# Last stage of a gated two-layer kernel: the choice of experts on 32 partitions, spread through DRAM, in place of TensorE transposes and pair products

## The chip, the cores and the metric

The kernel runs on one core of a Trainium2 chip. A core has five engines with their own instruction streams: TensorE (PE; its weight loads are shown apart as PEld), VectorE (DVE), ScalarE (ACT), GpSimd (POOL) and SyncE (SP), which here does nothing but issue DMA transfers, in order. Tensors lie in SBUF (128 partitions) or, for the results of TensorE, in PSUM banks. The metric is the device time of one execution in microseconds; lower is better.

## The reference, cut to what matters

All of it is float32, for 16 sequences ("batches") of 256 tokens with 256 channels. Two layers follow one another, each with a cross attention and a feed-forward part, each part added to `x` with a gate. The change concerns only the last part, a gated linear attention with a dense and a sparse half:

```python
e = jax.nn.softmax(x @ We, axis=-1)                   # 4 experts per token
_, idx = lax.top_k(e, 1)
mask = jax.nn.one_hot(idx, N_EXP, dtype=x.dtype).sum(-2)
rw = e * mask
fac = jnp.swapaxes(rw, 1, 2)[:, :, :, None, None]
mfac = jnp.swapaxes(mask, 1, 2)[:, :, :, None, None]
q_e = q2[:, None] * fac
k_e = k2[:, None] * fac
gk_e = gk2[:, None] * mfac
o_dense = gla_b(q1, k1, v, gk1)                       # chunked, causal
o_sparse = gla_be(q_e, k_e, v, gk_e).sum(axis=1)      # one attention per expert
o = o_dense + o_sparse
```

A pair of tokens (s, t) contributes to the sparse half only where both chose the same expert, and then with the product of the two tokens' probabilities; the decay (`gk_e`) between them sums only over tokens of that expert.

## The kernel before, in words

The kernel works through four stages, one per part, each with a loop over the 16 batches. The last one, `stage3_fast`, is a generator. Its first steps (for batch 0) are run between the steps of the stage before; then it runs a loop over p = 0 to 63, four quarters (m = 0 to 3) for each of 16 batches. Each quarter makes the keys, queries, decays and products of two heads of the dense and two of the sparse half. The instructions of this stage stay in the order in which the Python code issues them, on each engine; tables (`start`, `middle`, `rest`, `late`, `behind_mask`, `by_rows`, `logs`) name by quarter which preparatory step for the next batch is issued at which place of the quarter.

For the choice of experts of batch b + 1, made during batch b, these are:

- quarter 0: `lows` multiplies the normed tokens (`xnT`) with all low-rank weights and the four expert columns, so that PSUM holds the logits as rows 81 to 84, tokens along the free axis, and VectorE copies it to `low`. `route_rows` turns these rows with two TensorE transposes into a spare corner of the bank `sc`, so that tokens lie on partitions: 128 partitions, 2 token halves, 4 experts. `route_logits` subtracts the largest and takes the exponential, `route_sums` the reciprocal sum.
- quarter 1: `route` multiplies by it and finds the first largest of the 4 (ties are broken by `prio`, which falls from 4 to 1 along the experts), and writes `hots`: the probability at the chosen expert, 0 elsewhere.
- quarter 2: `turn_hot` turns `hots` with two TensorE transposes into 4 rows (`hT`), `turned_hot` copies them to SBUF.
- start of quarter 3: `pairs` multiplies `hT` with itself on TensorE (`both`, 256 + 128 columns). An entry is the product of two tokens' probabilities if they chose the same expert, else 0. VectorE makes two masks of it: `em` (is it above 0, times the decay mask `dmask`) and `am` (times the causal mask `amask`).

`em` is the moving operand of the `gz` products (`decays`), first needed for p + 1 in quarter 3. `am` is multiplied into the sparse products (`masked`, n = 1) from the next batch on.

Other work that these steps stand next to: `turn_ahead` (quarter 2) turns the normed tokens of batch b + 2 in 32x32 squares on VectorE into the tile `turned`, and SyncE puts the squares in place with 16 transfers into `xnT`, which `lows` reads in quarter 0 of the next batch. `norms` (quarter 1) sends the 8 rows of normalizing factors through DRAM (`rms`) and back, repeated over partitions (`r`, two transfers). `outgates` leaves copies in the tile tag `zs`. `steepest` reduces the logarithms of the gates (`gates`) in quarter 3, `project` multiplies with the output weights there (`proj`), and VectorE adds the result to `x`. There is one bank `sc` for the products: TensorE may write the next ones when VectorE's `at` has read the last.

In the profile all operations of VectorE, ScalarE and GpSimd in this stage carry line 50 (a helper), and TensorE's lines 1637 (matmul) and 1640 (transpose), so they are told apart by the names of their tiles.

Of the kernel before, what the change touches and what calls it, by code (L numbers as in the profile page):

```python
# [73 lines left out]
def layers(ctx: ExitStack, tc: tile.TileContext, t, out, check):  # L74
# [1544 lines left out]
    def stage3_fast(early_bank):  # L1619

        with ExitStack() as sx:
# [29 lines left out]
            hots = [w1.tile([P, 2, 4], F32, tag=f"hot{n}", name=f"hot{n}") for n in range(2)]  # L1651
# [43 lines left out]
            def lows(b):  # L1695

                low[b] = of(b).tile([P, 2, S], F32, tag="low", name="low")
                ps = bank("low")
                for c in range(2):
                    for k in range(2):  # L1700
                        matmul(ps[:, c * S:(c + 1) * S], la[:, k, c * P:(c + 1) * P], xnT[b][:, k, :],
                                         start=k == 0, stop=k == 1)
                dve3.tensor_copy(low[b][:, 0, :], ps[:, :S])
                dve3.tensor_scalar(low[b][:, 1, :], ps[:, S:], vec[:, V_ONE:V_ONE + 1], None, ALU.add)
                lowd[b] = of(b).tile([P, S], F32, tag="lowd", name="lowd")
                nc.sync.dma_start(out=lowd[b][64:], in_=low[b][:64, 1, :])
                if b > 0:
                    nc.sync.dma_start(out=low2, in_=low[b][64:, 1, P:])

            e_, den_, z_ = {}, {}, {}  # L1710

            def route_rows(b, ps):

                for i in range(2):
                    transpose(ps[:, 64 * i:64 * i + 64], low[b][64:P, 1, tokens(i)], ident[64:P, 64:P])
                z_["rt"] = ps

            def route_logits(b):

                ps = z_.pop("rt")  # L1720
                src = ps.rearrange("p (i e) -> p i e", i=2)[:, :, 17:21]
                mx = st.tile([P, 2], F32, tag="emx", name="emx")
                dve.tensor_reduce(mx, src, AX.X, ALU.max)
                e = e_[b] = st.tile([P, 2, 4], F32, tag="e", name="e")
                dve.tensor_tensor(e, src, bc(mx, [P, 2, 4], 2), ALU.subtract)
                act.activation(e, e, AF.Exp)

            def route_first(b):
                route_rows(b, bank("rt")[:, :P])
                route_logits(b)  # L1730

            def route_sums(b):
                den = den_[b] = st.tile([P, 2], F32, tag="eden", name="eden")
# [3 lines left out]
            def route(b):  # L1737
                e, shape = e_.pop(b), [P, 2, 4]
                dve.tensor_tensor(e, e, bc(den_.pop(b), shape, 2), ALU.mult)
                m, q, c = (st.tile(x, F32, tag=n, name=n) for n, x in (("em", [P, 2]), ("eq", shape), ("ec", [P, 2])))  # L1740
                dve.tensor_reduce(m, e, AX.X, ALU.max)
                first = bc(prio[:, 4:], shape, 1)
                dve.tensor_tensor(q, e, bc(m, shape, 2), ALU.is_equal)
                dve.tensor_tensor(q, q, first, ALU.mult)
                dve.tensor_reduce(c, q, AX.X, ALU.max)
                dve.tensor_tensor(q, q, bc(c, shape, 2), ALU.is_equal)
                dve.tensor_tensor(hots[b % 2], q, e, ALU.mult)
# [34 lines left out]
            def turn_hot(b):  # L1782
                ps = bank("hT")
                for i in range(2):
                    transpose(ps[:4, tokens(i)], hots[b % 2][:, i, :], ident)
                z_[b, "hot"] = ps

            def turned_hot(b):
                hT[b] = of(b).tile([4, S], F32, tag="hT", name="hT")
                dve3.tensor_copy(hT[b], z_.pop((b, "hot"))[:4, :S])  # L1790

            def pairs(b):

                x, both = hT.pop(b), bank("both")
                matmul(both[:, 0:S], x[:, :P], x, start=True, stop=True)
                matmul(both[:, S:3 * P], x[:, P:], x[:, P:], start=True, stop=True)
                em[b] = of(b).tile([P, 2, P], F32, tag="em", name="em")
                dve3.scalar_tensor_tensor(em[b], both.rearrange("p (i s) -> p i s", i=2)[:, :, :P], 0.0, dmask,
                                          ALU.is_gt, ALU.mult)
                am[b] = of(b).tile([P, 384], F32, tag="am", name="am")  # L1800
                dve3.tensor_tensor(am[b], both[:, :384], amask, ALU.mult)
# [104 lines left out]
            def products(p, n):  # L1906
# [4 lines left out]
                if n == 0 and m == 0 and b + 1 < B:  # L1911
                    route_rows(b + 1, ps[:, 1, 384:])
# [121 lines left out]


            start = {3: [(pairs, 1)]}
            middle = {0: [(lows, 1)], 1: [(all_gates, 1)], 2: [(turn_hot, 1)], 3: [(scaled_first, 0)]}

            rest = {0: [(bias, 2)], 2: [(turned_hot, 1), (norm_ahead, 2)], 3: [(steepest, 1, 0), (steepest, 1, 1)]}
# [15 lines left out]
            for group in (((bias, 0), (stats, 0)), ((norm, 0),), ((turn, 0),), ((lows, 0),), ((gates, 0, 0),),  # L2055
                          ((gate_logs, 0, 0), (route_first, 0)), ((route_sums, 0), (gates, 0, 1)),
# [6 lines left out]
            for f, *a in ((turn_hot, 0), (turned_hot, 0), (stats, 1), (pairs, 0), (norm, 1), (steepest, 0, 0),  # L2063
                          (steepest, 0, 1)):
                f(*a)
# [185 lines left out]
```

## Time and profile before

| | us |
|---|---|
| time, median of 3 runs | 1832.49 (1831.44 to 1832.76) |
| the profiled execution's own time | 1833.27 |
| its span, first to last instruction | 1831.5 |
| TensorE busy | 1793.7 |
| GpSimd busy | 1015.0 |
| VectorE busy | 1137.3 |
| ScalarE busy | 832.2 |

The granted TensorE clock was 0.997 of full speed. The last stage begins at about 1222 us of the span and takes about a third of it, 36.75 us for a batch. How to read the lines: in a view in order of time, the first number is the start from the beginning of the span, the second the time taken, then the engine, the line, the operation, output and inputs by tile name, their shapes (partitions x elements) and the number of instructions merged; in brackets the idle time of that engine before it and the instruction that ended it. In the chain that ended last, each piece is what the next one waited for, followed back from the last instruction of the kernel. TensorE's instructions run pipelined, and their ends are modelled, so they overlap in these lists.

### The profile page before, as it was taken

What the parts mean: (1) busy time and instruction counts of PE and PEld (TensorE: products, weight loads), DVE (VectorE), ACT (ScalarE), POOL (GpSimd) and SP (SyncE); (2) the same over time, 40 slices, a digit from 0 to 9 for tenths busy, and PEclk for the clock granted to TensorE, in tenths of its full rate; (3) what the DMA queues carried; (4) which work ended last, traced back from release to release, by engine and by line L of the source; (5) the groups of instructions that cost most, each with busy time, mean ns of one, the idle gap of its engine ahead of it and who ended that gap; (6) DMA issues with size and microseconds to landing.
All of it is one profiled execution on the core that took longest, in us unless ns stands there. A gap on an engine that the chain in (4) does not pass through costs nothing.

```text
span 1831.5 us, 35425 instructions
## 1 busy us (share of the span) xinstructions
PE 1793.7 (98%) x13930; PEld 1242.3 (68%) x13930; DVE 1137.3 (62%) x2695; ACT 832.2 (45%) x1727; POOL 1015.0 (55%) x1001
## 2 busy tenths in 40 slices
PE   8999999999999999999999999998999999999997
PEld 5666666666666666666777866656777777777775
DVE  3345656666656666666475388866666666666664
ACT  4433335343443334534343388754544454445432
POOL 3654766567666677656643866313454445444533
PEclk9999999999999999999999999999999999999999
DMA  9800010000010100000067933100111111111110
GB/s 303 231 1 22 16 35 13 28 17 16 31 35 10 30 20 10 28 24 17 13 207 244 256 64 50 24 3 11 35 30 36 29 31 34 34 31 27 38 31 26
DMA packets 110361, 98.05 MB, mean 54 GB/s; under 512 B 43835, under 2 KB 97763, under 8 KB 109673
## 3 DMA queue, kind: packets, MB, share of 16 engines
q1 hardware_dynamic: 97897, 78.91, 14.5%
q0 software_dynamic: 12288, 16.79, 4.5%
q8 instruction: 112, 1.84, 0.4%
q14 instruction: 64, 0.52, 0.1%
HBM read 52.03 MB, written 38.41 MB: 49 GB/s over the span
## 4 chain that ended last, share of the span: by engine, by line
PE 81%; DVE 7%; POOL 7%; ACT 2%; issue 2%; DMA 1%; SPq 0%; POOLq 0%; DVEq 0%; ACTq 0%
PE o L50 12%; PE qk L50 11%; PE v L50 9%; PE sc L50 8%; PE proj L50 7%; PE sc L1637 5%; PE kq L1637 5%; POOL es L50 4%; PE gq L1637 3%; PE v L1637 3%; PE proj L1637 3%; PE ex L50 3%; DVE at L50 2%; PE o L1637 2%; POOL rs L50 2%
## 5 line engine op out<-in xcount | busy, mean ns | idle before, releaser
L50 POOL TENSOR_SCALAR rs<-mv 128x2 f32<-128x2 f32 (+2 forms) x85 | 16.3, 191 | 398.3 <-DVE mv L50 396.5
L50 DVE RECIPROCAL rd<-o 128x256 f32<-128x256 f32 x64 | 112.3, 1755 | 155.9 <-PE o L50 155.9
L50 ACT ACTIVATE e<-sc 128x1024 f32<-128x1024 f32 (+1 forms) x192 | 181.6, 1016 | 18.4 <-PE sc L50 18.4
L50 POOL TENSOR_TENSOR at<-at,at 128x768 f32<-128x768 f32 x63 | 114.2, 1812 | 133.5 <-DVE at L50 133.5
L50 PE MATMUL sc<-qk 64*128 64x256 f32 (+1 forms) x1536 | 183.1, 384 | 0.5 <-DVE qk L50 0.5
L50 PE MATMUL o<-e,v 128*32 128x256 f32 (+1 forms) x3072 | 177.9, 379 | 0.0
L50 PEld LDWEIGHTS sc<-qk 64*128 64x128 f32 (+1 forms) x1536 | 132.0, 172 | 55.1 <-issue 26.8
L50 POOL TENSOR_TENSOR esum<-esum,es 128x512 f32<-128x512 f32 x128 | 163.4, 1277 | 10.0
L50 PE MATMUL qk<-kvT,wkv 128*128 128x333 f32 x512 | 164.3, 443 | 0.0
L50 POOL TENSOR_TENSOR es<-e 128x1024 f32<-128x1024 f32 x64 | 151.3, 2364 | 12.0 <-ACT e L50 9.0
L50 ACT ACTIVATE qk<-qk 128x256 f32<-128x256 f32 x128 | 48.8, 382 | 231.7 <-PE qk L50 231.7
L50 POOL TENSOR_TENSOR es<-es,e 77x1024 f32<-77x1024 f32 x64 | 150.3, 2349 | 5.0
L50 DVE TENSOR_TENSOR at<-sc,amask 128x768 f32<-128x768 f32 x64 | 61.3, 958 | 135.1 <-PE sc L1637 79.6
L50 PEld LDWEIGHTS o<-e,v 128*32 128x32 f32 (+1 forms) x3072 | 99.9, 110 | 66.2
L50 PE MATMUL qk<-kvT,wq 128*128 128x256 f32 x512 | 134.6, 385 | 0.0
L50 DVE COPY qk<-qk 128x333 f32<-128x333 f32 x128 | 64.6, 505 | 94.8 <-ACT qk L50 93.3
L50 POOL DMA_INDIRECT x<-rows_out,pos x64 | 100.9, 1577 | 35.8 <-issue 18.7
L50 PEld LDWEIGHTS qk<-kvT,wq 128*128 128x128 f32 x512 | 94.3, 189 | 35.1 <-issue 9.6
L50 PEld LDWEIGHTS qk<-kvT,wkv 128*128 128x128 f32 x512 | 97.2, 190 | 30.0
L50 PE MATMUL proj<-wo0h,oT 128*128 128x256 f32 x512 | 113.7, 380 | 0.3 <-DVE oT L50 0.3
L50 PE MATMUL v<-wkv,kvT 128*128 128x512 f32 x256 | 113.1, 595 | 0.0
L50 PEld LDWEIGHTS proj<-wo0h,oT 128*128 128x128 f32 x512 | 95.9, 190 | 13.9 <-issue 0.8
(267 smaller groups left out, 3919.5 us busy)
## 6 DMA issues: line engine op xcount, KB each, us to landing
rows<-zero SPq DMA_DIRECT2D x16, 640.0 KB
xin<-rows SPq DMA_DIRECT2D x16, 640.0 KB
r<-rms SPq DMA_DIRECT2D x30, 256.0 KB
rows_out<-y SPq DMA_DIRECT2D x16, 384.0 KB
v<-vctx SPq DMA_DIRECT2D x15, 308.0 KB
x<-in_x_dram SPq DMA_DIRECT2D x16, 256.0 KB
rows_out<-y SPq DMA_DIRECT2D x16, 256.0 KB
out_dram<-x SPq DMA_DIRECT2D x15, 256.0 KB
```

Of the source, the lines that this page charges most:

```text
L50: x = getattr(self.engine, name)(*a, **k)
L1637: tc.keep_in_program_order(nc.tensor.matmul(*a, **k))
```

## The change

The logits stay on 32 partitions. After `lows`, VectorE turns the 32 rows that hold the logits in 32x32 squares (`rl`, in a tile of the tag `turned`), so that a lane holds 8 tokens with 4 experts each. The choice is made there, on 32 lanes with 32 elements, and gives two numbers for each token: its largest probability (`w`) and the code of the expert that has it (`c`, from `prio`). One more VectorE transpose of a 32x32 square lays them out as rows, and a transfer writes them to DRAM (`picks`, 2 x 256 numbers). From there two transfers read them back: `rows`, both rows repeated on all 128 partitions (256 KB), and `cols`, where each partition gets the four numbers of its own two tokens.

The masks are then made on VectorE alone. `same` compares `c` along the free axis with `c` of the partition's own token and multiplies with `dmask`: two instructions of 128 elements. `weights` makes `am` as (same choice) times w, then times the own w and `amask`: four instructions, two of 256 and two of 128 elements. `pairs`, `turn_hot`, `turned_hot`, `route_rows` and the `hots` tiles are gone, with their TensorE and VectorE instructions. `same` stands where `pairs` stood, at the start of quarter 3, and `weights` after the two `steepest` reductions of quarter 3. For batch 0, at the start of the stage, `steepest` comes before `same` and `weights`, and the norm of batch 1 after them.

```diff
-            hots = [w1.tile([P, 2, 4], F32, tag=f"hot{n}", name=f"hot{n}") for n in range(2)]
+            choice, chosen = (w1.tile([P, 32], F32, tag=n, name=n) for n in ("choice", "chosen"))
+            nc.gpsimd.memset(choice, 0.0)
...
                 dve3.tensor_scalar(low[b][:, 1, :], ps[:, S:], vec[:, V_ONE:V_ONE + 1], None, ALU.add)
+                rl[b] = w1.tile([P, 4, P], F32, tag="turned", name="rl")[:, :2, :].rearrange("p x d -> p (x d)")
+                dve3.transpose(rl[b][64:96, :], ps[64:96, S:])
...
-            def route_rows(b, ps):
-
-                for i in range(2):
-                    transpose(ps[:, 64 * i:64 * i + 64], low[b][64:P, 1, tokens(i)], ident[64:P, 64:P])
-                z_["rt"] = ps
+            picks = [tc.dram_tile([2, S], F32, name=f"picks{b}") for b in range(B)]
+            few, own_rows = [32, 8, 4], slice(64, 96)
...
             def route(b):
...
-                dve.tensor_tensor(q, q, bc(c, shape, 2), ALU.is_equal)
-                dve.tensor_tensor(hots[b % 2], q, e, ALU.mult)
+                dve.transpose(chosen[own_rows], choice[own_rows])
+                nc.sync.dma_start(out=picks[b].rearrange("n (k a) -> (n k) a", a=32), in_=chosen[64:80])
+                x = w2.tile([P, 512], F32, tag="zs", name="rows") if b else w0.tile([P, 2, D], F32, tag="xn", name="rows")
+                rows[b] = x.rearrange("p (n s) -> p n s", n=2) if b else x
+                nc.sync.dma_start(out=rows[b], in_=bc(picks[b], [P, 2, S], 0))
+                cols_[b] = w1.tile([P, 2, 2], F32, tag="cols", name="cols")
+                nc.sync.dma_start(out=cols_[b], in_=picks[b].rearrange("n (i p) -> p n i", p=P))
...
-            def turn_hot(b):
-                ps = bank("hT")
+            def same(b):
+
+                em[b] = of(b).tile([P, 2, P], F32, tag="em", name="em")
                 for i in range(2):
-                    transpose(ps[:4, tokens(i)], hots[b % 2][:, i, :], ident)
-                z_[b, "hot"] = ps
-
-            def turned_hot(b):
-                hT[b] = of(b).tile([4, S], F32, tag="hT", name="hT")
-                dve3.tensor_copy(hT[b], z_.pop((b, "hot"))[:4, :S])
-
-            def pairs(b):
-
-                x, both = hT.pop(b), bank("both")
-                matmul(both[:, 0:S], x[:, :P], x, start=True, stop=True)
-                matmul(both[:, S:3 * P], x[:, P:], x[:, P:], start=True, stop=True)
-                em[b] = of(b).tile([P, 2, P], F32, tag="em", name="em")
-                dve3.scalar_tensor_tensor(em[b], both.rearrange("p (i s) -> p i s", i=2)[:, :, :P], 0.0, dmask,
-                                          ALU.is_gt, ALU.mult)
-                am[b] = of(b).tile([P, 384], F32, tag="am", name="am")
-                dve3.tensor_tensor(am[b], both[:, :384], amask, ALU.mult)
+                    dve3.scalar_tensor_tensor(em[b][:, i, :], rows[b][:, 1, tokens(i)], cols_[b][:, 1, i:i + 1],
+                                               dmask[:, i, :], ALU.is_equal, ALU.mult)
+
+            def weights(b):
+
+                w, c = (rows[b][:, n, :] for n in range(2))
+                x = am[b] = of(b).tile([P, 384], F32, tag="am", name="am")
+                for i, (lo, hi) in enumerate(((0, S), (S, 3 * P))):
+                    dve3.scalar_tensor_tensor(x[:, lo:hi], c[:, i * P:], cols_[b][:, 1, i:i + 1], w[:, i * P:],
+                                               ALU.is_equal, ALU.mult)
+                    dve3.scalar_tensor_tensor(x[:, lo:hi], x[:, lo:hi], cols_[b][:, 0, i:i + 1], amask[:, lo:hi],
+                                               ALU.mult, ALU.mult)
...
-                if n == 0 and m == 0 and b + 1 < B:
-                    route_rows(b + 1, ps[:, 1, 384:])
...
-            start = {3: [(pairs, 1)]}
-            middle = {0: [(lows, 1)], 1: [(all_gates, 1)], 2: [(turn_hot, 1)], 3: [(scaled_first, 0)]}
-
-            rest = {0: [(bias, 2)], 2: [(turned_hot, 1), (norm_ahead, 2)], 3: [(steepest, 1, 0), (steepest, 1, 1)]}
+            start = {3: [(same, 1)]}
+            middle = {0: [(lows, 1)], 1: [(all_gates, 1)], 3: [(scaled_first, 0)]}
+
+            rest = {0: [(bias, 2)], 2: [(norm_ahead, 2)], 3: [(steepest, 1, 0), (steepest, 1, 1), (weights, 1)]}
...
-            for f, *a in ((turn_hot, 0), (turned_hot, 0), (stats, 1), (pairs, 0), (norm, 1), (steepest, 0, 0),
-                          (steepest, 0, 1)):
+            for f, *a in ((stats, 1), (steepest, 0, 0), (steepest, 0, 1), (same, 0), (weights, 0), (norm, 1)):
```

More of the change, by code (lines that the diff above doesn't have):

```diff
@@ L1708, in lows, with small @@
                     nc.sync.dma_start(out=low2, in_=low[b][64:, 1, P:])
-            e_, den_, z_ = {}, {}, {}
-            def route_rows(b, ps):
-                for i in range(2):
-                    transpose(ps[:, 64 * i:64 * i + 64], low[b][64:P, 1, tokens(i)], ident[64:P, 64:P])
-                z_["rt"] = ps
+            e_, den_, z_, rl, rows, cols_ = {}, {}, {}, {}, {}, {}
+            picks = [tc.dram_tile([2, S], F32, name=f"picks{b}") for b in range(B)]
+            few, own_rows = [32, 8, 4], slice(64, 96)
+            def small(name, shape):
+                return w1.tile([P] + shape[1:], F32, tag=name, name=name)[own_rows]
             def route_logits(b):
-                ps = z_.pop("rt")
-                src = ps.rearrange("p (i e) -> p i e", i=2)[:, :, 17:21]
-                mx = st.tile([P, 2], F32, tag="emx", name="emx")
+                src = rl.pop(b)[own_rows].rearrange("p (k c) -> p k c", c=32)[:, :, 17:21]
+                mx = small("emx", few[:2])
                 dve.tensor_reduce(mx, src, AX.X, ALU.max)
-                e = e_[b] = st.tile([P, 2, 4], F32, tag="e", name="e")
-                dve.tensor_tensor(e, src, bc(mx, [P, 2, 4], 2), ALU.subtract)
+                e = e_[b] = small("e", few)
+                dve.tensor_tensor(e, src, bc(mx, few, 2), ALU.subtract)
                 act.activation(e, e, AF.Exp)
-            def route_first(b):
-                route_rows(b, bank("rt")[:, :P])
-                route_logits(b)
             def route_sums(b):
-                den = den_[b] = st.tile([P, 2], F32, tag="eden", name="eden")
+                den = den_[b] = small("eden", few[:2])
                 dve.tensor_reduce(den, e_[b], AX.X, ALU.add)
@@ L1737, in route @@
             def route(b):
[L1738 to L1744, printed above, removed]
-                dve.tensor_reduce(c, q, AX.X, ALU.max)
-                dve.tensor_tensor(q, q, bc(c, shape, 2), ALU.is_equal)
-                dve.tensor_tensor(hots[b % 2], q, e, ALU.mult)
+                e, q = e_.pop(b), small("eq", few)
+                w, c = choice[own_rows, :8], choice[own_rows, 8:16]
+                dve.tensor_tensor(e, e, bc(den_.pop(b), few, 2), ALU.mult)
+                dve.tensor_reduce(w, e, AX.X, ALU.max)
+                dve.tensor_tensor(q, e, bc(w, few, 2), ALU.is_equal)
+                dve.tensor_tensor(q, q, bc(prio[own_rows, 4:], few, 1), ALU.mult)
+                dve.tensor_reduce(c, q, AX.X, ALU.max)
+                dve.transpose(chosen[own_rows], choice[own_rows])
[5 more added lines that the diff above has]
+                nc.sync.dma_start(out=cols_[b], in_=picks[b].rearrange("n (i p) -> p n i", p=P))
             def gates(b, i):
@@ L2055, in stage3_fast @@
             for group in (((bias, 0), (stats, 0)), ((norm, 0),), ((turn, 0),), ((lows, 0),), ((gates, 0, 0),),
-                          ((gate_logs, 0, 0), (route_first, 0)), ((route_sums, 0), (gates, 0, 1)),
+                          ((gate_logs, 0, 0), (route_logits, 0)), ((route_sums, 0), (gates, 0, 1)),
                           ((route, 0), (vals, 0), (gate_logs, 0, 1), (bias, 1))):
```

## The prediction

> **What bounds the kernel now.** I read the page's busy times, the chain that ended last over one batch of the last stage, then VectorE, SyncE and TensorE in order of time over that batch.
>
> ```profile
> PE 1793.7 (98%) x13930; PEld 1242.3 (68%) x13930; DVE 1137.3 (62%) x2695; ACT 832.2 (45%) x1727; POOL 1015.0 (55%) x1001
> ```
>
> TensorE is busy 98% of the span: work taken from it is worth its time, unless something else was nearly as late. The chain over 1487 to 1525 (start us, us, what):
>
> ```profile
> 1495.54 0.27 PE sc L1640
> ...
> 1496.69 0.96 DVE at L50
> 1497.65 0.08 DVE emx L50
> ...
> 1497.95 0.21 ACT e L50
> ...
> 1498.68 1.29 DVE zs L50 x2
> ...
> 1500.57 1.30 DVE at L50 x4
> ...
> 1501.91 0.70 PE sc L1637 x2
> ...
> 1509.62 0.22 PE hT L1640 x2
> ...
> 1517.11 0.84 PE both L1637 x4
> ```
>
> A batch takes 36.75 us (`low` starts at 1492.74 and 1529.50). The three routing pieces of TensorE (turned logits 0.27, `hT` 0.22, `both` 0.84) all lie on the chain. In quarter 0 the chain leaves TensorE for VectorE, through the routing operations `emx`, `e` and `eden`, and comes back at 1501.91. VectorE in quarter 3 (idle time before, and its releaser, in brackets):
>
> ```profile
> 1517.22 0.41 DVE L50 TENSOR_TENSOR q<-gq,ee 128x256 f32<-128x256 f32 x1
> 1517.99 0.42 DVE L50 SCALAR_TENSOR_TENSOR em<-both,dmask 128x256 f32<-128x256 f32 x1 [0.37 <-PE both L1637]
> 1518.34 0.55 DVE L50 TENSOR_TENSOR am<-both,amask 128x384 f32<-128x384 f32 x1
> 1518.80 1.38 DVE L50 SCALAR_TENSOR_TENSOR at<-sc,kden,am 128x256 f32<-128x256 f32 x4
> 1520.10 0.68 DVE L50 TENSOR_TENSOR u<-o,gw 128x512 f32<-128x512 f32 x1
> 1520.70 2.33 DVE L50 TENSOR_REDUCE gates<-lg 128x1 f32<-128x1024 f32 x2
> 1524.27 0.75 DVE L50 SCALAR_TENSOR_TENSOR x<-proj,gate,x 128x512 f32<-128x512 f32 x1 [1.24 <-PE proj L1637]
> ```
>
> It has 1.24 us of air before `x<-proj`. SyncE, and the TensorE instruction its sixteen `xnT` transfers are for:
>
> ```profile
> 1508.42 1.32 SPq L1998 DMA_DIRECT2D r<-rms  x2
> ...
> 1516.79 10.33 SPq L1693 DMA_DIRECT2D xnT<-turned  x16
> ```
> ```profile
> 1272.12 1.97 PE L1637 MATMUL low<-xnT,la 128*128 128x256 f32 x8 [1.68 <-DMA xnT<-turned]
> ...
> 1529.50 1.89 PE L1637 MATMUL low<-xnT,la 128*128 128x256 f32 x8
> ```
>
> The last issue ends at 1527.12, `low` starts 2.38 us later. Where `low` did wait, it started 1.37 to 1.54 us after the last issue (1270.58 to 1272.12, 1748.92 to 1750.29): I take 1.4, so the usual slack is about 0.98 us. This second path, from VectorE's `turned` over SyncE to the next `low`, decides how much of the gain can be kept.
>
> **The change part by part.** The sum is made against the profiled execution's 1833.27 us (span 1831.5), 0.78 above the median of 1832.49.
>
> *Quarter 0 (15 batches).* The turned logits leave TensorE: -0.27. VectorE's new 32x256 transpose sits between the `low` copies (end 1495.48) and `at`; priced by `dens` (128x256, 0.44) it ends at 1495.9, before `at` can start at 1496.42: hidden, with its cover 0.5 us. If it weren't, `at` would be late one for one. The small operations now have 32 elements a lane in place of 8. From 128 to 256 elements `at` goes from 342 to 472 ns, about 1 ns an element, so 24 elements cost 25 ns each for `emx`, `e`, `eden`; the exponential 20 (128x8 is 208); the reciprocal goes from 166 ns (2 elements) to 244 (16), 5.6 ns an element, so 34 for 6 more. They follow one another on the chain: +0.13. Net -0.14, ends -0.27 (nothing added) and 0 (twice as much added). 15 x 0.14 = 2.1.
>
> *Quarter 1.* `route` loses two operations of 0.19 and gains 25 ns on five and a 32x32 transpose (128x64 takes 0.239): the same end within 0.1 us. GpSimd waits for the `mv` behind it, but its `at` sum ends 0.6 us before TensorE's `o` at 1515.03: nothing. SyncE gets three issues: `picks` waits for `chosen`, `rows` for the landing of `picks`, `cols` follows. Queued behind them are only the sixteen `xnT` issues at 1516.8, and SyncE is free from 1509.74.
>
> *Quarter 2.* `hT` leaves TensorE: 15 x 0.22 = 3.3. TensorE runs without a pause from there to `sc`, and the 0.40 VectorE copy lay in idle time.
>
> *When do rows and cols land?* `rms` (8 KB to DRAM) took 1.74 us from issue to release. `picks` is issued at 1509.74 behind the two `r` transfers, whose data flows until 1512.4, so it lands at about 1512.9. `rows` (256 KB) then starts moving about 1.4 us after its issue (as `r` did) and takes half of what the two `r` took, 1.2: until 1515.5. `cols` is 512 pieces of 4 bytes, 32 on each of the 16 DMA engines. No row has 4-byte pieces. Lower end: the first load, `vec`, has pieces of 72 bytes, 143 packets in 9.5% of 16 engines over 1 us, 10.6 ns each: 0.35 us. Upper end: `r` with 1 KB pieces, 512 packets in 2.6 us at 0.69 of 16 engines, 56 ns: 1.8 us. With 0.45 us to release, `cols` is there between 1516.3 and 1517.8. I take the lower end, `vec` being the nearest in size. VectorE reaches `same` at 1517.41 (its `q`, 0.22 earlier).
>
> [...]
>
> *Quarter 3, TensorE.* `both` goes: -0.84. *VectorE* loses `em` and `am` (0.97 together and 0.37 of waiting). New: operations with a lane scalar cost 0.342 (128 elements) and 0.472 (256); independent ones start 0.09 before the last ends, dependent ones 0.03 after. `same`: 2 x 0.25 = 0.50. `weights`: 0.50 + 0.38 + 0.37 + 0.25 = 1.5. From 1517.41: GpSimd's `u` product still runs until 1517.57, and I let `same` wait for it, because both its operands lie in SBUF: earlier, `rq<-re,prio` of one form ran from 160 to 2189 ns, one of them (888.60, 1.07 us) ending with GpSimd's pair of sums (887.03, 2.62 us). Then 1517.57 + 0.50 + `at` 1.30 + `u` 0.60 + `gates` 2.33 + 1.5 = 1523.8. `x<-proj` could start at 1523.19, so it is 0.6 late; `at` ends at 1525.44, just when TensorE wants its `sc` bank (1525.44). So VectorE's air is used up, and nothing is lost yet; any further lateness of `same` is paid one for one.
>
> [...]
>
> *Quarter 3, what is late next.* `turned` comes before `both`, so its landing doesn't move, while `low` would come 0.84 earlier. Slack per batch (end of the last issue to `low`, less 1.4): seven batches 0.91 to 0.99, six with longer issuing (10.65 to 11.35 us) 0.51, 0.66, 0.41, 0.27, 0.03 and 0; the first has none (it waits 1.68 already). The last batch has no `low`. Kept: 7 x 0.84 + 1.9 + 0 + 0.84 = 8.6 of 12.6. Ends: 12.6 if SyncE is never late, 4 if its 3 more issues a batch lengthen the seven too.
>
> *Start of the stage.* Route ends at 1220.2 now and `em` at 1226.34. Then: 0.26 earlier without the turned logits, picks 1.74, rows 0.65 + 1.4 + 1.2, cols 0.35 + 0.45, landing near 1225.8, while `gates`, now ahead, ends near 1226.2. `em` ends at 1226.7, +0.3 with ends -0.3 and +1.0 (`cols` at 56 ns). `weights` and `xn` behind it (2.2 us) end before TensorE's `tr` at 1231.
>
> Sum: 2.1 + 3.3 + 8.6 - 0.3 = 13.7. 1833.27 - 13.7 = 1819.6, on the median's scale 1818.8.
>
> **The rivals.**
> - *All of it.* The transfers of `xnT` keep up: 15 x (0.14 + 0.22 + 0.84) - 0.3 = 17.7, giving 1814.8 (1812.8 with nothing added to the small operations). For it: seven batches still have 0.14 us over. Against it: six have less than 0.84.
> - *VectorE is the bound in quarter 3.* `weights` blocked by GpSimd or dearer, or `cols` at its upper end (1517.8, 0.2 late): 0.2 to 0.8 us a batch. The first 0.14 hides under the `xnT` slack; 1820 to 1829.
> - *Slower: the 4-byte pieces are dear.* `same` waits for `cols`, VectorE stands, and `gz` and the `sc` bank are late. A batch gains 0.36 before it and 0.84 in it, so it decides from 1.2 us of lateness: landing 1518.8, (1518.8 - 0.45 - 1515.5) / 32 = 89 ns a piece. At 100 ns the landing is 1519.15, 1.6 late, 0.4 lost a batch: 1832.5 + 6 + 0.3 = 1839. For it: no row shows such a piece. Against it: both priced rows lie below.
> - *The pieces leave TensorE and nothing shortens*: excluded, since they lie on the chain without a pause.
>
> **How the numbers follow.** Forecast 0.50 (1815.5 to 1821); all of it 0.12 (1812 to 1815.5); VectorE the bound 0.19 (1821 to 1829); slower or near no change 0.19 (0.03 of it within 0.2%, which is 3.7 us and about what a measurement can tell). The range 1812.5 to 1829 leaves out the last case. Faster 0.78, same 0.04, slower 0.18.
>
> **What would show it.** Right: no `both`, `hT` or turned logits; batches of about 35.7 to 36.0 us; `low` waiting for `xnT` in some; `same` starting within 0.2 us of `q`'s end; `x<-proj` with no idle time before it. Wrong: VectorE's `em` waiting for `cols` by a microsecond or more; `cols`' issue on SyncE well above 0.7 us; TensorE idle at the second `sc` of quarter 3; `xnT` issues starting later than 0.1 us after `turned`.

## The result: 0.23% slower

| | before | after |
|---|---|---|
| time, median of 8 runs each, one chip (us) | 1832.11 (1828.88 to 1834.36) | 1836.56 (1834.65 to 1838.77) |
| ratio to before, 95% interval | | 1.0023 [1.0013, 1.0033] |
| the profiled execution's own time | 1833.27 | 1837.53 |
| its span | 1831.5 | 1835.7 |
| granted TensorE clock | 0.997 | 0.995 |

The forecast was 1818.8 us, with a range of 1812.5 to 1829: too low by 17.8 us, with the sign wrong. TensorE did lose the work: between the second batch's `low` and the last one it was busy 504.09 us before and 492.21 after, but that stretch took 514.41 us before and 519.12 after. So its idle time there grew from 10.3 to 26.9 us. The busy times on the page of the kernel after:

```profile
PE 1778.2 (97%) x13802; PEld 1226.5 (67%) x13802; DVE 1165.8 (64%) x2743; ACT 834.1 (45%) x1727; POOL 1014.6 (55%) x1002
```

Four marks on TensorE divide a batch: the first `low`, the first of the gate products (`sc<-lbg`, whose bank VectorE's `at` has to free), the first `v`, the first `proj`, and the next `low`. Summed over the 13 batches that have all five, in us:

| kernel | low to gate products | to v | to proj | to next low | sum |
|---|---|---|---|---|---|
| before | 119.46 | 112.63 | 130.44 | 115.64 | 478.17 |
| after | 125.21 | 109.74 | 124.51 | 122.62 | 482.08 |
| difference | +5.75 | -2.89 | -5.93 | +6.98 | +3.91 |

With the batch before these (36.24 to 37.04, +0.80) and what follows the last `low` (81.2 to 80.7, -0.5), that is the 4.2 us between the spans. Two stretches gain, two lose more. The clock does not explain it: the granted clock is 1.00 over these 13 batches in both executions. In the batch before them it is 0.50 for 3.41 us after the change (1268.93 to 1272.34), and from `den` to `low` takes 4.0 us there instead of 2.4; before, `low` waited 1.68 us for `xnT` in that batch, so the two nearly cancel.

Of the 3.91 us, 3.0 fall in two neighbouring batches of after (37.74 and 38.79 us in place of 36.76), which the last section looks at: in each, a packet of 16 KB of the queue `q8 instruction` moved (for 1.28 and 1.43 us) while a transfer was on its way. In the other eleven, gains and losses nearly cancel: 0.9 us in all.

**The first stretch.** The chain that ended last, kernel after, at the same place as the lines of before (start us, us, what):

```profile
1494.59 1.97 PE low L1637 x8
...
1498.41 0.97 DVE at L50
...
1504.25 0.70 PE sc L1637 x2
```

The turned logits, `hT` and `both` are gone; the path over VectorE, through `emx`, `e` and `eden`, is still there, and longer. From `low` to `at` it is 3.82 us (3.95 before, 1492.74 to 1496.69), but from `at` to the gate products 5.84 (5.22 before, 1496.69 to 1501.91). VectorE itself in order of time, kernel before and kernel after:

```profile
1496.69 0.96 DVE L50 TENSOR_TENSOR at<-sc,amask 128x768 f32<-128x768 f32 x1 [1.21 <-PE sc L1637]
1497.56 0.15 DVE L50 TENSOR_REDUCE emx<-sc 128x2 f32<-128x8 f32 x1
1497.75 0.17 DVE L50 TENSOR_TENSOR e<-sc,emx 128x8 f32<-128x8 f32 x1
1497.84 0.68 DVE L50 TENSOR_TENSOR f<-kq,ee 128x512 f32<-128x512 f32 x1
```
```profile
1498.41 0.96 DVE L50 TENSOR_TENSOR at<-sc,amask 128x768 f32<-128x768 f32 x1 [0.53 <-PE sc L1637]
1499.40 0.18 DVE L50 TENSOR_REDUCE emx<-rl 32x8 f32<-32x32 f32 x1
1499.62 0.18 DVE L50 TENSOR_TENSOR e<-rl,emx 32x32 f32<-32x32 f32 x1
1499.83 0.69 DVE L50 TENSOR_TENSOR f<-kq,ee 128x512 f32<-128x512 f32 x1
...
1501.92 0.41 DVE L50 TENSOR_TENSOR q<-gq,ee 128x256 f32<-128x256 f32 x1
1502.36 0.18 DVE L50 TENSOR_REDUCE eden<-e 32x8 f32<-32x32 f32 x1
1502.57 0.19 DVE L50 RECIPROCAL eden<-eden 32x8 f32<-32x8 f32 x1
1502.80 1.39 DVE L50 SCALAR_TENSOR_TENSOR at<-sc,kden,am 128x256 f32<-128x256 f32 x4
```

The small operations themselves cost next to nothing more (0.18 and 0.19 in place of 0.15 to 0.17). What is new is at the seams: `emx` starts 0.03 us after `at` ends, `f` 0.03 after `e`, `eden` 0.03 after `q`, `at` 0.04 after the reciprocal. None of these pairs depends on one another, and in the kernel before they overlapped by 0.08 to 0.09 (`at` 1496.69 + 0.96 = 1497.65, `emx` at 1497.56; `e` 1497.75 + 0.17 = 1497.92, `f` at 1497.84). At just these four places the operations change between tiles that begin at partition 64 and tiles that begin at partition 0.

**The end of a batch.** SyncE in order of time, kernel after, one batch (its `low` began at 1420.47):

```profile
1436.62 1.33 SPq L1994 DMA_DIRECT2D r<-rms  x2
1438.04 0.55 SPq L1744 DMA_DIRECT2D picks<-chosen  x1
1442.11 0.35 SPq L1747 DMA_DIRECT2D rows<-picks  x1
1442.51 0.43 SPq L1749 DMA_DIRECT2D cols<-picks  x1
1444.78 11.27 SPq L1694 DMA_DIRECT2D xnT<-turned  x16
```

TensorE and VectorE in the quarter 3 that follows:

```profile
1444.29 0.82 PE L1637 MATMUL sc<-q,k 64*128 64x256 f32 x8
1445.35 1.13 PE L1637 MATMUL kq<-xnT,wk 128*128 128x256 f32 x4 [0.24 <-DVE f L50]
1448.07 3.62 PE L1637 MATMUL proj<-wo,u 128*128 128x256 f32 x16
...
1457.64 1.97 PE L1637 MATMUL low<-xnT,la 128*128 128x256 f32 x8 [0.38 <-DMA xnT<-turned]
```
```profile
1444.02 0.70 DVE L50 STREAM_TRANSPOSE turned<-xn 128x512 f32<-128x512 f32 x1
1444.64 0.65 DVE L50 TENSOR_TENSOR f<-kq,ee 128x512 f32<-128x512 f32 x1
1445.22 0.41 DVE L50 TENSOR_TENSOR q<-gq,ee 128x256 f32<-128x256 f32 x1
1445.93 0.61 DVE L50 SCALAR_TENSOR_TENSOR em<-rows,cols,dmask 128x128 f32<-128x128 f32 x2 [0.30 <-DMA cols<-picks]
...
1452.18 0.75 DVE L50 SCALAR_TENSOR_TENSOR x<-proj,gate,x 128x512 f32<-128x512 f32 x1
1452.84 0.95 DVE L50 TENSOR_TENSOR at<-sc,amask 128x768 f32<-128x768 f32 x1
```

Three things are late here. `kq` waits for `f`, which has to free the only `kq` bank and stands behind `turned`; while `both` stood in front of `kq`, it gave `f` that time. `em` waits for `cols`. And `low` waits for the transfers of `xnT`: from `turned` to `low` it takes 13.62 us here (1444.02 to 1457.64) and 13.48 in the kernel before (1479.26 to 1492.74). With 23.28 us from `low` to `turned` before (1455.98 to 1479.26) the path adds up to the period of 36.76, as it must; what counts is the slack in it. Before, the sixteen issues took 10.34 us and ended 2.38 us ahead of `low`, of which about 1.4 is needed (so much where `low` did wait). After, the path is 23.55 (1420.47 to 1444.02) + 13.62 = 37.17: the issues take 11.27 us and end 1.59 us ahead of `low` (1456.05 to 1457.64), so no slack is left. Whatever TensorE gained behind `turned` cannot shorten that.

### The profile page after: what moved, and what is told of

Its sections match the earlier page's. It is cut to its first block, busy times and chain, and to the rows that moved or that the text cites. A ratio compares the mean times of both kernels' runs of the same rounds, so it can differ in the third digit from the quotient of the medians.

```text
span 1835.7 us, 35258 instructions
## 1 busy us (share of the span) xinstructions
PE 1778.2 (97%) x13802; PEld 1226.5 (67%) x13802; DVE 1165.8 (64%) x2743; ACT 834.1 (45%) x1727; POOL 1014.6 (55%) x1002
## 4 chain that ended last, share of the span: by engine, by line
PE 73%; DVE 10%; POOL 7%; DMA 2%; ACT 2%; issue 2%; SPq 2%; DVEq 0%; POOLq 0%; ACTq 0%
PE o L50 11%; PE qk L50 11%; PE v L50 9%; PE sc L50 8%; PE proj L50 7%; PE sc L1637 5%; PE kq L1637 4%; POOL es L50 4%; DVE at L50 3%; PE ex L50 3%; PE v L1637 2%; PE gq L1637 2%; PE proj L1637 2%; PE low L1637 2%; POOL rs L50 2%
```

## The experiments

The theory at this point: (1) the change of partitions costs VectorE's overlap, 0.6 us a batch on the way to the gate products; (2) the transfers of `xnT` eat what is gained behind `turned`; (3) if they are made faster, VectorE's `f` and its lateness in quarter 3 come next. Rivals: the small operations are dear for their shape; the wait for `cols` is the cause; the two DRAM steps slow everything that SyncE issues. All runs below have the kernel before timed beside them on the same chip (medians 1830.92 to 1832.35 us); the groups ran on four chips, so runs of different groups are best compared by their ratios or by the sums over the 13 batches.

### Choice on partitions 0 to 31

```diff
-                dve3.transpose(rl[b][64:96, :], ps[64:96, S:])
+                dve3.transpose(rl[b][0:32, :], ps[64:96, S:])
...
-            few, own_rows = [32, 8, 4], slice(64, 96)
+            few, own_rows = [32, 8, 4], slice(0, 32)
...
-                nc.sync.dma_start(out=picks[b].rearrange("n (k a) -> (n k) a", a=32), in_=chosen[64:80])
+                nc.sync.dma_start(out=picks[b].rearrange("n (k a) -> (n k) a", a=32), in_=chosen[0:16])
```

> The changed kernel, with the choice on partitions 0 to 31 in place of 64 to 95 (the transpose of the logits writes there). Theory 1: quarter 0 got slower (from `low` to the gate products 9.66 us in place of 9.17) because VectorE stops overlapping two operations whenever the first partition changes between 0 and 64, which it does four times on that path at 0.11 to 0.12 us. Then this stretch falls to about 9.2 us, the `f` after `e` starts before `e` has ended again, and the time falls by 15 x 0.46 = 6.9 us, to about 1829.7. Rival: the small operations cost that much because of their 32 elements a lane or because both operands lie in SBUF; then the stretch stays at 9.6 and the time at 1836.5.

Measured: 1826.15 us, ratio 0.9970 [0.9958, 0.9981]: faster than before. From `low` to the gate products: 117.66 us in the 13 batches (9.05 each), in place of 125.21. The stretch gains 0.58 us a batch where 0.46 had been expected. The time is 3.5 us below the expected 1829.7; this explains 1.8 of it, and the rest is not explained. VectorE in order of time in this run:

```profile
1313.26 0.96 DVE L50 TENSOR_TENSOR at<-sc,amask 128x768 f32<-128x768 f32 x1 [0.53 <-PE sc L1637]
1314.13 0.16 DVE L50 TENSOR_REDUCE emx<-rl 32x8 f32<-32x32 f32 x1
1314.33 0.18 DVE L50 TENSOR_TENSOR e<-rl,emx 32x32 f32<-32x32 f32 x1
1314.44 0.67 DVE L50 TENSOR_TENSOR f<-kq,ee 128x512 f32<-128x512 f32 x1
...
1316.49 0.41 DVE L50 TENSOR_TENSOR q<-gq,ee 128x256 f32<-128x256 f32 x1
1316.82 0.16 DVE L50 TENSOR_REDUCE eden<-e 32x8 f32<-32x32 f32 x1
1317.02 0.19 DVE L50 RECIPROCAL eden<-eden 32x8 f32<-32x8 f32 x1
1317.14 1.33 DVE L50 SCALAR_TENSOR_TENSOR at<-sc,kden,am 128x256 f32<-128x256 f32 x4
```

The same instructions with the same shapes, and the four seams overlap again by 0.07 to 0.09 us: `at` to the next `at` takes 3.88 us in place of 4.39. The four seams alone are 0.13 + 0.31 = 0.44 of that 0.51. Shape was not the cause, the start partition was: with the change between 64 and 0 the four pairs stood 0.03 to 0.04 us apart, without it they overlap. No run tried the choice on other partitions.

### Four of the sixteen transfers of xnT issued by ScalarE

```diff
-                for q in range(0, P, 32):
+                for q in range(0, 96, 32):
...
+            def turn_rest(b):
+                to, y = z_.pop((b, "turned"))
+                for r in range(0, P, 32):
+                    tc.keep_in_program_order(nc.scalar.dma_start(out=to[r:r + 32, :, 96:], in_=y[96:, :, r:r + 32]))
...
-                    2: [(gate_logs, 1, 1), (normed_out, -1, 0), (normed_out, -1, 1)]}
+                    2: [(gate_logs, 1, 1), (turn_rest, 2), (normed_out, -1, 0), (normed_out, -1, 1)]}
```

Three kernels carry this edit: after with it, after with it and partitions 0 to 31, and before with it.

> The changed kernel, with 4 of the 16 `xnT` transfers of each batch issued by ScalarE after its gate logarithm of quarter 2, so that SyncE issues 12. Theory 1: in quarter 3 the next `low` waits for these transfers, whose path from `turned` to `low` is 13.4 to 13.6 us before and after the change, so that none of the 0.53 us gained on TensorE is kept. Then the stretch from `proj` to `low` falls from a mean of 9.4 us to the 8.89 of before, `low` waits for nothing, and the time falls by 14 x 0.5 = 7 us, to about 1829.5. Rival: quarter 3 is held by VectorE, whose `weights` push `x<-proj` and `at` back; then TensorE waits at the second `sc` of quarter 3, the stretch stays above 9.2 us, and the time stays within 2 us of 1836.5.

> Both edits together: choice on partitions 0 to 31, and 4 of 16 `xnT` transfers issued by ScalarE. Theory 1 (two separate causes): the gains add, a batch takes about 36.05 us, and the time is about 1822.6, below that of before. If only one of them is a cause, about 1829.5; if neither, 1836.5.

> The kernel before, with 4 of 16 `xnT` transfers issued by ScalarE. Theory 1: before the change these transfers held `low` up only in the first batch (1.68 us) and by some tenths in the last ones, so the time falls by about 2 us, to 1830.5. If they were a bound in every batch before the change already, it falls by 5 us or more, and then what the split gives to the changed kernel says nothing of the change.

Measured: after with it 1832.29 us, 0.9999 [0.9991, 1.0008]; with both edits 1824.02, 0.9950 [0.9936, 0.9963]; before with it 1829.77, 0.9990 [0.9980, 0.9999]. TensorE's waits between 1270 and 1750 us, kernel after and kernel after with the split (in all, times, longest, us):

```profile
PE sc L1637 <- DVE at L50: 15.2, 15, 1.1
PE kq L1637 <- DVE f L50: 3.1, 13, 0.2
PE low L1637 <- DMA xnT<-turned: 2.2, 4, 1.1
```
```profile
PE sc L1637 <- DVE at L50: 17.4, 17, 1.9
PE kq L1637 <- DVE f L50: 3.1, 13, 0.2
```

`low` waits for nothing now; from `proj` to `low` falls from 122.62 to 118.90 us, not to before's 115.64. Part of the wait has gone over to `at`, which is VectorE, but less than the two lists seem to say: 1.9 of the 17.4 us is a wait at 1269.93, which in the kernel after came at 1268.06, ahead of the window. Counted from `proj`, the `sc` that waits for `at` in quarter 3 comes 2.4 us late in all over the 13 batches, and 1.7 without the split. So (2) holds, but the split after is slower than I had expected by 2.8 us, and the last 3.3 us need another cause. In the kernel before, the split touches only the first of these intervals (36.24 to 34.40 us); every other batch stays at 36.76.

### Cols ahead of rows

```diff
-                nc.sync.dma_start(out=rows[b], in_=bc(picks[b], [P, 2, S], 0))
                 cols_[b] = w1.tile([P, 2, 2], F32, tag="cols", name="cols")
                 nc.sync.dma_start(out=cols_[b], in_=picks[b].rearrange("n (i p) -> p n i", p=P))
+                nc.sync.dma_start(out=rows[b], in_=bc(picks[b], [P, 2, S], 0))
```

On top of both edits above.

> The kernel with the choice on partitions 0 to 31 and the split xnT load (1824.0 us), with the cols transfer issued before the rows transfer. Theory (the column load itself is short, and em waits because cols stands behind the 256 KB of rows): cols is issued about 0.4 us earlier and no longer shares its engines with rows, em waits for cols nowhere but in the late batch, and the 3 to 4.7 us of waiting become 1.5 or less; since VectorE has some air there the time moves by 0 to -2 us, 1822 to 1824. Rival (the 512 pieces of 4 bytes are what takes the time): cols lands as late as before (3.4 us after its issue, less 0.4), and rows, now behind the pieces, lands later by 1 us or more, so that same waits for rows instead: 1824 to 1832.

Measured: 1823.76 us, 0.9963 [0.9950, 0.9976]: no difference. `em` now waits for `rows`, 6.9 us in 11 batches, where it had waited 4.6 us for `cols` in 7. It starts 3.5 to 3.8 us after the issue of the second transfer, as before (3.3 to 3.5). So where `em` waits for them, the pair of transfers takes 3.8 to 3.9 us in one order and 4.0 to 4.2 in the other: the order isn't what counts. The trace shows the pieces themselves. DMA queues of the kernel after from 1445.2 to 1445.5 us, in the batch whose `low` began at 1420.47:

```profile
DMA packets 269, 0.00 MB, mean 10 GB/s; under 512 B 268, under 2 KB 268, under 8 KB 269
...
q1 hardware_dynamic: 269, 0.00, 50.0%
```

Half of what 16 engines have in 0.3 us, for 269 packets: 9 ns each. So the load by pieces is short, as the theory had it, and the rival is wrong. What takes the time is `rows`: its 128 packets of 2 KB move from 1.0 to 3.2 us after its issue in this batch, and the pieces come among the last of them and behind, until 3.4. With `cols` ahead, `em` waits for `rows` instead.

### The turn behind the factors

```diff
-            behind_mask = {0: [(route_logits, 1)], 2: [(turn_ahead, 2)]}
-            by_rows = {0: [(outgates, 0)], 1: [(gates_end, 1)]}
+            behind_mask = {0: [(route_logits, 1)]}
+            by_rows = {0: [(outgates, 0)], 1: [(gates_end, 1)], 2: [(turn_ahead, 2)]}
```

> The kernel with the choice on partitions 0 to 31 and the split xnT load (1824.0 us), with the two operations that turn xn for the next batch moved from before the product f to after the factors that f feeds, in quarter 2 of VectorE. Theory (TensorE's first matmul of quarter 3 waits for f, which frees the one kq bank, and f comes about 0.3 us too late because the turn stands ahead of it): the wait of kq for f goes, from v to proj takes 9.2 in place of 9.50 us, 15 x 0.3 = 4.5 us, 1819.5 us; the later turn costs nothing, since the split load has over 2 us of slack. Rival (kq is late for something else, or the next wait stands as close behind): from v to proj stays above 9.4, 1823 to 1825, or low waits for xnT again and proj to low grows above 9.2.

Measured: 1823.99 us, 0.9955 [0.9942, 0.9968]: no gain. The wait of `kq` for `f` is gone and from `v` to `proj` takes 9.19 us, before's 10.03 less exactly 0.84; but from `proj` to `low` grows from 118.92 to 122.87 us, more than what `v` to `proj` won (123.69 to 120.46). With the split in place it is not `xnT` that holds `low`, but `at` in front of it: VectorE's work in quarter 3 is as long as the quarter, and TensorE merely waits at another place.

### Weights in quarter 0

```diff
-            middle = {0: [(lows, 1)], 1: [(all_gates, 1)], 3: [(scaled_first, 0)]}
+            middle = {0: [(weights_late, 0), (lows, 1)], 1: [(all_gates, 1)], 3: [(scaled_first, 0)]}
...
-            rest = {0: [(bias, 2)], 2: [(norm_ahead, 2)], 3: [(steepest, 1, 0), (steepest, 1, 1), (weights, 1)]}
+            rest = {0: [(bias, 2)], 2: [(norm_ahead, 2)], 3: [(steepest, 1, 0), (steepest, 1, 1)]}
```

`weights_late` calls `weights` for all batches but the first. On top of the late turn; the second kernel has `cols` ahead of `rows` as well.

> As the one before with the late turn, and with the four weights operations of the next batch moved from the end of VectorE's quarter 3 to its quarter 0, ahead of the low copies. Theory (what is left of VectorE's lateness at the end of quarter 3 is the 1.5 us of weights ahead of x<-proj and of at): proj to low is 8.89 in all but the late batch, 1 to 3 us below the kernel with the late turn alone, 1817 to 1819. Rival (the weights are then in the way of the low copies or of the first at of quarter 0, where VectorE has no air either): low to gate products grows from 9.0 by 0.2 to 0.6 a batch, 3 to 9 us slower than the late turn alone.

> All four edits: choice on partitions 0 to 31, split xnT load, late turn, late weights, and cols issued before rows. If they add: 1816 to 1818. If the weights rival holds, near 1823; if the rows behind cols come too late, 0.2 to 0.8 us a batch more than the kernel with late weights.

Measured: 1826.87 us, 0.9979 [0.9970, 0.9988], and 1827.47, 0.9979 [0.9970, 0.9988]. From `proj` to `low` is 8.89 us in all batches, so VectorE's lateness was the cause there. From `low` to the gate products is 10.08 in place of 9.01, and the groups by line show why. VectorE's between 1270 and 1510 us (busy us, mean ns of one), and GpSimd in order of time at one such place, kernel with the late weights:

```profile
L50 DVE SCALAR_TENSOR_TENSOR am<-rows,cols 128x256 f32<-128x256 f32 x6 | 9.5, 1591 | 0.0
L50 DVE SCALAR_TENSOR_TENSOR am<-am,cols,amask 128x256 f32<-128x256 f32 x6 | 9.3, 1554 | 0.2
```
```profile
1448.56 1.81 POOL L50 TENSOR_TENSOR at<-at,at 128x768 f32<-128x768 f32 x1 [5.73 <-DVE at L50]
...
1450.70 1.26 POOL L50 TENSOR_TENSOR x<-x,gbo 128x512 f32<-128x512 f32 x1
```

At their old place these two took 0.47 to 0.49 us each in the kernel after; in the kernel with the late turn the first took 0.63 to 0.84 in four of 13 batches. Here the first starts at 1449.07, inside GpSimd's sum, and ends at 1450.66, 0.29 after it; the second starts at 1450.69, just before GpSimd's next sum, and ends 0.28 after that one. Both of their tensors lie in SBUF, as GpSimd's do. This is the wait for GpSimd that the prediction had allowed for in quarter 3; here it cost 1.1 us per instruction (1.59 and 1.55 in place of 0.47 to 0.49).

### One reduction in quarter 0, and picks issued by ScalarE

```diff
-            middle = {0: [(lows, 1)], 1: [(all_gates, 1)], 3: [(scaled_first, 0)]}
+            middle = {0: [(steepest_late, 0), (lows, 1)], 1: [(all_gates, 1)], 3: [(scaled_first, 0)]}
...
-            rest = {0: [(bias, 2)], 2: [(norm_ahead, 2)], 3: [(steepest, 1, 0), (steepest, 1, 1), (weights, 1)]}
+            rest = {0: [(bias, 2)], 2: [(norm_ahead, 2)], 3: [(steepest, 1, 0), (weights, 1)]}
```

On top of the late turn, with the weights back in quarter 3; `steepest_late` is `steepest(b, 1)` for all batches but the first. In the second kernel ScalarE issues `picks`:

```diff
-                nc.sync.dma_start(out=picks[b].rearrange("n (k a) -> (n k) a", a=32), in_=chosen[0:16])
+            def spread(b):
+                tc.keep_in_program_order(nc.scalar.dma_start(out=picks[b].rearrange("n (k a) -> (n k) a", a=32), in_=chosen[0:16]))
...
-                    1: [(route, 1), (stats, 2), (outgates_end, 0, 1), (gate_logs, 1, 0)],
+                    1: [(route, 1), (stats, 2), (outgates_end, 0, 1), (gate_logs, 1, 0), (spread, 1)],
```

> The kernel with the choice on partitions 0 to 31, the split xnT load and the late turn (1824.0 us, where from proj to low takes 9.0 to 10.2 us), with one of the two reductions gates of 1.17 us moved from VectorE's quarter 3 to quarter 0 of the next batch, ahead of the low copies, where VectorE stood still for 2.1 us. Theory (TensorE waits at the end of quarter 3 for at because VectorE has 0.1 to 0.6 us too much to do there): from proj to low takes 8.89 in all batches but the late one; TensorE's waits for at are 14.2 us in all, of which 15 x 0.5 belong to quarter 0, so some 5 to 6 us go: 1818 to 1819.5. A reduction has one operand in SBUF, so it isn't held by GpSimd's sum as the two products of weights were there (1.59 and 1.55 in place of 0.48 us). Rival (anything VectorE does at that place delays the low copies, as weights did): from low to the gate products grows above 9.1, and the time stays at 1823 or more.

> As the one before, with the picks transfer issued by ScalarE after the first gate log of quarter 1, while rows and cols stay with SyncE. It tells what the 3.2 to 4.4 us from the issue of picks to the issue of rows are. If picks stands behind the 512 KB of the two r transfers in SyncE's queue: rows is issued 1 to 2 us earlier, em waits for cols in no batch but the late one, and the time is 0 to 2 us below the kernel with the late reduction. If it is the way to DRAM and back itself: about 3.9 us again, em's waits stay near 5 us in all, and the time is within 1 us of it.

Measured: 1814.99 us, 0.9908 [0.9892, 0.9925], and 1814.96, 0.9903 [0.9888, 0.9918]. Ten of the 13 batches of the first kernel take 35.53 us, which is 36.76 - 1.23. TensorE's waits between 1270 and 1750 us, and VectorE at the new place, kernel with the late reduction:

```profile
PE sc L1637 <- DVE at L50: 7.3, 15, 0.5
PE gz L1637 <- DVE em L50: 0.5, 1, 0.5
```
```profile
1447.18 1.16 DVE L50 TENSOR_REDUCE gates<-lg 128x1 f32<-128x1024 f32 x1
1449.35 0.42 DVE L50 COPY low<-low 128x256 f32<-128x256 f32 x1 [1.01 <-PE low L1637]
```

The reduction ran beside a GpSimd sum (1446.68, 1.81 us) without being held (it took 1.16 there, 1.21 at its old place in the kernel with the late turn). In quarter 3 of the same trace the other reduction took 1.21 (at 1438.61) beside the sum at 1438.17 (1.82 us), and the first two products of `weights` behind it, with two SBUF operands, took 0.54 and 0.83 (at 1439.73 and 1440.31): each ended 0.28 after the GpSimd operation that it had begun beside (that sum, and the 0.91 us from 1439.95). No run tried the number of operands alone. Behind the reduction in quarter 0, VectorE still stood for 1.01 us before the copies of `low`. The gain is larger than expected (9.0 us below the run with the late turn). 6.1 us of it come from nearly every batch losing its lateness: from `proj` to `low` 122.87 to 116.81 us. Another 3.2 come from the batch before the 13 (37.36 to 34.12 us): in it, the profiled execution with the late turn had two stretches of 3.41 us at a granted clock of 0.50 (from 1244.26 and 1268.15), this one none. Whether the edit or chance took them away is not shown.

With `picks` in ScalarE's queue it no longer stands behind `r` in program order and is issued about 1 us earlier in the batch (15.9 us after `low`, not 16.9). But `rows` is still issued 3.1 to 3.8 us after it, against 3.6 to 4.6; at the start of the stage, before the first `r`, it is 1.4 in both. So a separate queue was worth a few tenths; the rest was there in the batches, where other data moves, and not at the start. The packets in the traces show it: at the start of the stage the 16 packets of `picks` move 0.8 to 1.0 us after the issue; in the kernel after, behind `r`, they move between 1.5 and 3.8 us after it and end with the last packets of `r`. `em` waits for `cols` in no batch any more, and the late batch takes 35.70 in place of 36.91 us, yet the time is the same: the wait of `em` had become nearly harmless.

### The same edits without the change, and without its other partitions

The first kernel is the one before with split, late turn and late reduction; the second is after with these three, and the choice on partitions 64 to 95.

> The kernel before, with the three edits that do not belong to the change: split xnT load, late turn, one reduction gates in quarter 0 of the next batch. Theory (before has no late wait for them to remove: from low to low 36.76 us is TensorE's own work in all batches, and the edits help only where the change has left TensorE less to do than VectorE and SyncE): the split's gain in the first batches alone, 1829 to 1830.5 us. Rival (the edits are worth their gain by themselves, and the change adds nothing to it): 1821 or less.

> The kernel after with the same three edits, and the choice on partitions 64 to 95 as the change has it. Theory (each change of the start partition costs VectorE its overlap, 0.6 us a batch, on the way to the gate products, whatever the rest of the batch does): from low to the gate products takes 9.6 in place of 9.01 us, 15 x 0.58 = 8.7 us above the kernel with partitions 0 to 31 (1815.0), 1823.7. Rival (with the late reduction VectorE has air for it there): from low to the gate products below 9.3, 1815 to 1819.

Measured: 1830.40 us, 0.9995 [0.9983, 1.0007], and 1823.11, 0.9957 [0.9943, 0.9970]. Before has nothing to win from these edits: 36.75 to 36.77 us in 12 of the 13 batches, TensorE's own but for 0.46 us in which it waits for `at` ahead of the gate products. So most of what the edits bring is there only with the change: alone it loses 0.23%, on partitions 0 to 31 it gains 0.30%, and with the three edits as well 0.92%. With them, the start partition is worth 8.1 us (1823.11 - 1814.99, on two chips; 7.1 in the 13 batches): 9.58 in place of 9.01 us from `low` to the gate products.

## Why the prediction was wrong, by its own steps

Two steps failed. *Quarter 0* forecast -0.14 us a batch and measured +0.44 on the mean: it put at nothing what the new start partition does to the neighbours. *Quarter 3, what is late next* forecast that 8.6 of 12.6 us would be kept; over the 13 batches 1.05 us were lost, mainly because it sized the slack of the path over SyncE too large. One by one:

- **Quarter 0** (net -0.14 per batch, ends -0.27 and 0): it came out at +0.41 to +0.49, outside both ends. "They follow one another on the chain: +0.13" priced the longer lanes only; that term is right within a few hundredths. The overlap lost at four seams was not in it, though the prediction itself used "independent ones start 0.09 before the last ends" a few lines on. Of the 0.27 of the turned logits 0.13 was seen. The new transpose was hidden, as forecast.
- **Quarter 2** (`hT`, -0.22): 8.66 to 8.44 us, right.
- **When rows and cols land** (1516.3 to 1517.8, or 23.6 to 25.1 us after `low`): `cols` let `em` start 25.46 after `low` in the batch shown, of which 0.49 is quarter 0. Nearer the upper end than the lower, which I had taken. The pieces were not what was mis-sized: they took 9 ns, and the lower end had 10.6. `picks` took 3.6 to 4.5 us to the next issue in most batches where 3.2 had been forecast, with its packets among the data of `r`, and `rows` moved for about 2.1 us, not 1.2. The wait cost `em` 0.2 to 0.3 us in most batches.
- **Quarter 3, TensorE** (-0.84): -0.53, and -0.84 once the turn was moved. The step looked at TensorE's instructions and not at the bank that `kq` needs; `both` was the cover of `f`.
- **Quarter 3, VectorE** ("nothing is lost yet"): wrong by a little, in a place where every tenth counts. With `xnT` out of the way (partitions 0 to 31, split), seven of the 13 batches still lost 0.1 to 0.7 us from `proj` to `low`, beside the late one; with one of the two reductions moved away as well, only three lost anything, the late one among them.
- **What is late next** (kept 8.6 of 12.6 us, ends 4 and 12.6): the mechanism was right, the size was not. Over quarter 3 and its end the 13 batches lost 1.05 us (-5.93 + 6.98). The slack of 0.9 us was read off seven batches with an issue burst of 10.3 us; after, nine of 13 bursts took 10.7 to 11.4, against six before, and `turned` itself came 0.27 later after `low`. About 3.8 of the 6.98 us fell in these nine batches, 2.5 in the two disturbed ones of the last section, 0.5 in one where `at` was late. The three added issues did not lengthen the burst: the four short ones of after took 10.34 to 10.35 us. I had given the case "all lengthened" a lower end of 4 us, when it is a loop: `low` to `turned`, `turned` to `low`, in which TensorE gains only the turned logits and `hT`, and quarter 0 takes more than that away.
- **Start of the stage** (+0.3): `low` of the second batch at 1235.89, before 1235.88: nothing.

The rival that ended slower, dear 4-byte pieces, named the wrong cause: the kernel was slower without `cols` being 1.2 us late in more than one batch, and with pieces of 9 ns. Of the four signs of being wrong, none showed in most batches; the seams were not among them. "VectorE is the bound in quarter 3" was true as a second limit behind `xnT`. "All of it" (1814.8 us) is close to what the change can give: with partitions 0 to 31, the split, the late turn and the late reduction it is 1815.0. That the two agree to 0.2 us is partly chance: against the kernel before with the same three edits (0.9908 / 0.9995), the change is worth 0.87%, about 16 of the 17.7 us of that rival.

## What to carry to other kernels

Price a small operation by what it does to its neighbours too: look at the partition where its tiles begin, and whether the operation before and after it begin at another (here 0.44 us a batch at four seams). When work leaves the busiest engine, follow every loop that returns to the same instruction (here `low` to `turned` over SyncE back to `low`) and add up the loop, not the slack of its typical turn; and ask of each removed instruction which wait it had been covering. Where room has to be made on VectorE beside GpSimd, try an operation with one SBUF operand first: here the reduction took 1.16 us beside GpSimd's sum, 1.21 at its old place, and the products with two took 1.59 and 1.55 in place of 0.47 to 0.49.

## What the runs showed of the hardware that was not expected

- Neighbouring VectorE operations that do not depend on each other overlapped by 0.07 to 0.09 us in the kernel before and with the choice on partitions 0 to 31, and by nothing (0.03 to 0.04 apart) in the kernel after, at the four places where the start partition changes between 64 and 0: about 0.11 us per change, 0.4 to 0.5 us per batch.
- The burst of sixteen SyncE issues took 10.32 to 10.35 us or 10.65 to 11.4, in the kernels before and after. All nine long ones of after and five of the six of before have a packet of the queue `q8 instruction` within them; none of the short ones has. No run here tried whether it is the cause.
- In every kernel with the new transfers one batch, between 1518 and 1571 us, has the 8 KB of `rms` land late, by 1.5 to 2.1 us. Kernel after:

```profile
1546.73 0.60 SPq L1991 DMA_DIRECT2D rms<-rs  x1
1550.39 1.33 SPq L1994 DMA_DIRECT2D r<-rms  x2
```

`r` is issued when `rms` has landed, 3.66 us after its issue; in other batches it is 1.74. That batch takes 38.79 us, where the others take 36.4 to 37.7. The kernel before does not show it, and issuing `picks` from another queue left it in place for `rms` (3.87). The DMA queues between the two issues show what is special there:

```profile
q8 instruction: 1, 0.02, 2.2%
q1 hardware_dynamic: 16, 0.01, 0.9%
```

One packet of q8, of 16 KB, moved from 1.16 to 2.43 us after the issue of `rms`. Seven of the eight packets of `rms` began 1.24 to 1.30 us after it; the eighth began at 2.42, as that packet ended. So it is in all eleven kernels with the new transfers: the eighth packet begins at 2.05 to 2.62 us, as such a packet of q8 ends, and in no other of the 13 batches does one move between the packets of `rms` and the issue of `r`. The batch before is the other one of the two: `low` waits 1.08 us at 1532.32 for transfers of `xnT` that were all issued by 1529.24. A packet of q8, of 16 KB, moved from 1529.7 to 1531.1, and the last eight packets of `xnT`, of 128 bytes, came behind it. No run moved the packets of q8, so that they would fall elsewhere in another version of the kernel is an expectation, not shown.
